# Turning a decoder's tokens through DRAM and VectorE's 32x32 squares, and the last step of a norm on GpSimd

## The chip, the cores and the metric

The kernel runs on one core of a Trainium2 chip. The metric is the device time of one execution in microseconds (us). Five engines work side by side, each with its own queue of instructions in a fixed order: TensorE (PE in the profile; its weight loads are PEld), VectorE (DVE), ScalarE (ACT), GpSimd (POOL) and SyncE (SP), which here issues nearly all DMAs. An engine's instruction waits until what it needs from others is there, and all that stands behind it in its queue waits too.

## The reference

Two decoder layers on 16 sequences of 128 tokens, 512 features wide, in float32. Each sublayer is followed by a sum and a norm without weights:

```python
x = _layernorm(x + _L0_attn_ref(x, ...))            # softmax attention, 16 heads over 4 key heads, rotary
x = _layernorm(x + _L0_xattn_ref(x, ctx_512, ...))  # latent cross attention, 16 heads of 128
x = _layernorm(x + _L0_ffn_ref(x, w1, w2, w3))      # gated FFN with ternary weights, 1408 wide
x = _layernorm(x + _L1_attn_ref(x, ...))            # lightning (decay) attention, 16 heads of 32
x = _layernorm(x + _L1_xattn_ref(x, ctx_512, ...))  # causal softmax cross attention, 16 heads of 32
x = _layernorm(x + _L1_ffn_ref(x, ...))             # 8 experts, two for each token, and a shared expert

def _layernorm(x, axis=-1, eps=1e-05):
    m = jnp.mean(x, axis=axis, keepdims=True)
    v = jnp.var(x, axis=axis, keepdims=True)
    return (x - m) / jnp.sqrt(v + eps)
```

## The kernel before

**Tiling.** The tokens stay in on-chip memory through all six stages as 16 tiles `x[b]` ("blocks") of 128 tokens by 512 features, tokens on the partitions. A projection contracts over features, so it needs them on the partitions: a block is turned into four squares of 128x128, written `xT[:, k, at : at + P]`, k being 0 to 3. Blocks go in groups of four (`GB = 4`, `NG = 4` groups); `xT` holds a group, 4 x 512 values on each partition. Before the change every block is turned by four TensorE transposes into a bank of PSUM and one ACT copy out of it (`transpose_x`, L125 to L130; stage 3 has its own at L673).

**Stages and their order.**

- *Stage 1*, softmax self attention. `attend` (L229) runs over the blocks, n counting up: scores of block n on TensorE; their softmax, where VectorE takes maxima (L188), ACT the exponentials (L193), GpSimd the division (L200); the turning of the probabilities of block n - 1 on TensorE (L205) with a copy by VectorE (L207); values and output projection of block n - 2 (`project_out`, L146). The projections of the next group are a list of tasks with costs in microseconds, made by `prepare(g)`; a `Share` deals them out between these steps by their cost, so that TensorE has them to do while it waits for a softmax. `prepare` also appends `folds`: products of cross attention weights of stage 2, whose raw tensors (`raw`, 1.7 MB each) come by SP.
- *Stage 2*, latent cross attention, runs over (group, half of the heads, block). `context` (L535) fetches a group's latent keys and values from DRAM (`rep`, from `dkv`, which `rotate` wrote), turns them and the group's tokens; `project` makes queries and keys for a half; `Heads` does softmax and values. Ternary weights of stage 3 are made in between (`pieces`).
- *Stage 3*, the FFN. For each group, 11 chunks f of hidden units: 16 matmuls (L697) with the tokens split into a high and a low part (`xh`, `xl`), then the product with the third matrix. The turning of the next group (`inputs`, `one`) hangs in a list `todo`, one item in each chunk.
- *Stage 4*, decay attention. For each group: turning, eight pieces of queries and keys (L785), values (L793); then each block goes through a `Pipeline` of scores, values and `project_out`.
- *Stage 5*, softmax cross attention, is `attend` again, with its own `prepare` (L891). It also loads shared weights for stage 6, and at its start has SP write 20 MB of zeros to DRAM (`slots_x`, `sums`, L900).
- *Stage 6*, the experts, is not touched.

**Norm.** `statistics` (L110) takes mean and variance on VectorE, and the reciprocal root on GpSimd (L116, L118); `layernorm` then has VectorE do the last step (L123). `project_out` of stages 1, 4 and 5 calls it, and so do stages 2 and 3.

Order within an engine is the program's, unless a scheduler moves an instruction that is ready sooner; `tc.keep_in_program_order` forbids that for one instruction. Tiles with the same `tag` share `bufs` rooms: a new tile waits until the oldest has been read for the last time.

Of the kernel before, what the change touches and what calls it, by code (L numbers as in the profile page):

```python
# [12 lines left out]
F32 = mybir.dt.float32  # L13
F32R = mybir.dt.float32r
AF = mybir.ActivationFunctionType
ALU = mybir.AluOpType
# [29 lines left out]
def decoder_kernel(ctx: ExitStack, tc: tile.TileContext, a: dict, out: bass.AP):  # L46
# [71 lines left out]
        nc.gpsimd.tensor_tensor(rstd, ve, nhalf, ALU.pow)  # L118
        return mv[:, 0:1], rstd

    def layernorm(b):
        mean, rstd = statistics(b)
        nc.vector.tensor_scalar(x[b], x[b], mean, rstd, ALU.subtract, ALU.mult)  # L123

    def transpose_x(xT, b, at):  # L125

        tr = bank("mm", [P, KC, P], "tr")
        for k in range(KC):
            nc.tensor.transpose(tr[:, k, :], x[b][:, k * P : (k + 1) * P], ident)
        nc.scalar.copy(xT[:, :, at : at + P], tr)  # L130

    def chain(tasks, name, pairs, then):

# [179 lines left out]
    with tc.tile_pool(name="p1", bufs=1) as p1:  # L313
# [85 lines left out]
        def prepare(g):  # L399
            if g == NG:  # L400
                room = p1.tile([P, KC, TG], F32, tag="xT", name="room")
                ct, t2 = (room[:, n].rearrange("p (b d) -> p b d", d=DC) for n in range(2))
                return [(0, rotate(0, ct, kvr0, t2))] + folds(2, LATE)
            xT = p1.tile([P, KC, TG], F32, tag="xT", name="xT")
            qkT = p1.tile([P, 5, TG], F32, tag="qkT", name="qkT", bufs=2)
            v = p1.tile([P, GB, P], F32, tag="v", name="v", bufs=2)
            groups[g] = qkT, v
            tasks = []

            def turn(i):  # L410
# [3 lines left out]
            tasks += [(0.64, lambda i=i: turn(i)) for i in range(GB)]  # L414
# [92 lines left out]
    with tc.tile_pool(name="p2", bufs=1, reuse_waits="tile") as p2:  # L507
# [27 lines left out]
        def context(g, kvr):  # L535
            reps = []
            for i in range(GB):
                rep = p2.tile([P, 4, DC], F32, tag="rep", name="rep", bufs=GB + 1)
                for qi in range(4):
                    nc.sync.dma_start(  # L540
                        rep[qi * Q : (qi + 1) * Q], dkv[g * GB + i].rearrange("(kj k) d -> k kj d", k=Q)
                    )
                reps.append(rep)
            pk = bank("mm", [P, GB, P], "pk")
            for i in range(GB):
                nc.tensor.transpose(pk[:, i, :], kvr[:, i, :], ident)
            kvT = p2.tile([P, TG], F32, tag="kvT", name="kvT")
            nc.scalar.copy(kvT, pk.rearrange("p b l -> p (b l)"))
            xT = p2.tile([P, KC, TG], F32, tag="xT", name="xT")
            for i in range(GB):  # L550
                transpose_x(xT, g * GB + i, i * P)
            return xT, kvT, reps

        def project(xT, kvT, half):
            qT = p2.tile([P, 4, TG], F32, tag="qT", name="qT")
# [65 lines left out]
                    if self.half == 1:  # L621
                        layernorm(self.b)

        kvr = kvr0
# [7 lines left out]
        for m in range(len(steps) + 2):  # L632
            if m < len(steps):
                g, half, i = steps[m]
                if i == 0:
                    if half == 0:
                        xT, kvT, reps = context(g, kvr)
# [5 lines left out]
                if (half, i) == (1, 1) and g + 1 < NG:  # L643
                    kvr = p2.tile([P, GB, DC], F32, tag="kvr", name="kvr")
                    rotate(g + 1, room("ct"), kvr, room("t2"))()
# [17 lines left out]
    with tc.tile_pool(name="p3", bufs=1) as p3:  # L663
        w1, w2 = (tern.w[n].rearrange("p (k f) -> p k f", k=KC) for n in range(2))
        def inputs(g):
            xh = p3.tile([P, KC, TG], F32R, tag="xh", name="xh", bufs=2)
            xl = p3.tile([P, KC, TG], F32R, tag="xl", name="xl", bufs=2)

            def one(i):
                at = slice(i * P, (i + 1) * P)  # L670
                tr = bank("mm", [P, KC, P], "tr")
                for k in range(KC):
                    nc.tensor.transpose(tr[:, k, :], x[g * GB + i][:, k * P : (k + 1) * P], ident)  # L673
                nc.scalar.copy(xh[:, :, at], tr)
                nc.vector.tensor_tensor(xl[:, :, at], tr, xh[:, :, at], ALU.subtract)
            return (xh, xl), [lambda i=i: one(i) for i in range(GB)]

        xs, todo = inputs(0)
        for run in todo:
# [4 lines left out]
        for g in range(NG):  # L684
# [51 lines left out]
    with tc.tile_pool(name="p4", bufs=1) as p4:  # L736
# [28 lines left out]


        pipe = Pipeline((0, 1, 2))
        for g in range(NG):
            xT = p4.tile([P, KC, TG], F32, tag="xT", name="xT", bufs=2)
            for i in range(GB):  # L770
                transpose_x(xT, g * GB + i, i * P)
                nc.gpsimd.tensor_tensor(x[g * GB + i], x[g * GB + i], bo4, ALU.add)
            if g == 0:
                for j in range(4):
                    dj = p4.tile([P, 4, P], F32, tag=f"dec{j}", name=f"dec{j}")
                    for c in range(4):
                        h = 4 * c + j
                        nc.scalar.activation(dj[:, c, :], diff, AF.Exp, scale=nsl[:, h : h + 1])
                    nc.gpsimd.tensor_tensor(dj, dj, bc(maskT, 4), ALU.mult)
                    dec.append(dj)  # L780
            qkT = p4.tile([P, 8, TG], F32, tag="qkT", name="qkT", bufs=2)
            for c in range(8):
                pq = bank("mm", [P, TG], "pq")
                for k in range(KC):
                    nc.tensor.matmul(  # L785
                        pq, lhsT=wq4[k // 2][:, k % 2, c * P : (c + 1) * P], rhs=xT[:, k, :], start=(k == 0), stop=(k == KC - 1)
                    )
                nc.scalar.activation(qkT[:, c, :], pq, AF.Identity, bias=bcol[:, c : c + 1])
            vs = []
            for i in range(GB):  # L790
                pv = bank("mm", [P, D], "pv")
# [5 lines left out]
                v = p4.tile([P, D], F32, tag="v", name="v", bufs=6)  # L797
                nc.vector.tensor_tensor(v, pv, bv4, ALU.add)
                vs.append(v)
            for i in range(GB):  # L800
                toks = slice(i * P, (i + 1) * P)
                mine = {}

# [67 lines left out]
    with tc.tile_pool(name="p5", bufs=1) as p5:  # L871
# [12 lines left out]
        nc.gpsimd.iota(count[:, NC + NB :], [[P, NT]], base=NB * P, channel_multiplier=1)  # L884
        ramp = moe.tile([P, NC + NB + NT], F32, tag="ramp", name="ramp")
        nc.vector.tensor_copy(ramp, count)
        wq5, wo5 = wqo5[:, 0], wqo5[:, 1]
        psum.share(mm=2, sc=4, pt=2)
        groups = {}

        def prepare(g):  # L891
# [12 lines left out]
            xT = p5.tile([P, KC, TG], F32, tag="xT", name="xT", bufs=2)  # L904
# [22 lines left out]
            for i in range(GB):  # L927
                chain(
                    tasks, "pv", [(ctT[:, i * P : (i + 1) * P], wkv5[:, D : 2 * D])],
                    lambda pv, i=i: nc.scalar.copy(vs[i], pv),  # L930
                )
            return tasks

        def score(sc, n):
# [487 lines left out]
```

## Time and profile before

| | us |
|---|---|
| median of three runs (lowest, highest) | 2133.3 (2128.42, 2134.7) |
| the profiled execution | 2133.8 |
| its span, first to last instruction | 2132.0 |
| TensorE's mean granted clock in it, as a share of full speed | 0.991 |
| stage 1, self attention | 0 to 266 |
| stage 2, latent cross attention | 266 to 767 |
| stage 3, FFN | 767 to 1021 |
| stage 4, decay attention | 1021 to 1291 |
| stage 5, softmax cross attention | 1291 to 1546 |
| stage 6, experts | 1546 to 2132 |

The ends of stages are read from the timeline and are good to a microsecond or two, as neighbouring stages overlap. In the profile's lines, "x64" counts instructions, "128x512 f32" is partitions by elements, and a bracket such as `[1.63 <-POOL rstd L118]` is the idle time of that engine just before the instruction and what ended it. L123 is line 123 of the kernel before. Of the lines that concern the turning: L129, TensorE's transposes of tokens outside stage 3, 320 instructions of 273 ns (they overlap one another); L673, the same in stage 3, 64 instructions; L130, ACT's copy of a turned block, 80 of 585 ns; L123, the norm's last step, 80 of 547 ns at the median.

### The profile page before, as it was taken

Reading aid. Unit: us, or ns where it says so; the run is one execution under the profiler, and the core shown is the slowest. Engines: PE = TensorE matmul, PEld = TensorE weight load, DVE = VectorE, ACT = ScalarE, POOL = GpSimd, SP = SyncE. Lnnn points to the kernel's source line nnn. Section 1 sums busy time; section 2 is a strip of 40 time slices with the busy share of each in tenths; the row PEclk is TensorE's granted clock in tenths of the full one; section 3 lists DMA queues with packets and bytes.
Section 4 is the critical chain, followed back from the end, with each engine's and each line's share of the span. In section 5 each row is a group of like instructions: output and inputs, shape, how many; then the busy total and the mean of one; then the engine's idle time right before and its main releaser. Section 6 shows DMA issues by size and latency. Waiting matters only on the chain.

```text
span 2132.0 us, 26951 instructions
## 1 busy us (share of the span) xinstructions
PE 2077.3 (97%) x10273; PEld 1170.9 (55%) x10273; DVE 865.6 (41%) x1776; ACT 642.6 (30%) x2252; POOL 540.9 (25%) x626
## 2 busy tenths in 40 slices
PE   8999999999999999999999999999799999999998
PEld 5555554445454468888455544555444455555553
DVE  4677733444554343322124424677631122222224
ACT  4555533323333322222211113566431111111112
POOL 5443321211111122222211101333303212222223
PEclk9999999999999999999999999999899999999999
DMA  6001220212220010001200029300004268999874
GB/s 227 1 34 44 103 85 22 63 46 70 60 70 1 1 54 1 1 1 60 93 1 1 1 50 301 140 21 21 26 16 164 83 214 293 292 298 304 297 216 165
DMA packets 82896, 210.05 MB, mean 99 GB/s; under 512 B 19792, under 2 KB 38096, under 8 KB 76112
## 3 DMA queue, kind: packets, MB, share of 16 engines
q0 software_dynamic: 13792, 105.55, 15.1%
q1 hardware_dynamic: 67872, 101.47, 14.5%
q8 instruction: 81, 1.33, 0.3%
q10 hardware_dynamic: 1104, 1.31, 0.2%
q14 instruction: 47, 0.39, 0.1%
HBM read 159.70 MB, written 48.61 MB: 98 GB/s over the span
## 4 chain that ended last, share of the span: by engine, by line
PE 90%; DVE 4%; DMA 2%; ACT 1%; POOL 1%; issue 1%; ACTq 0%; POOLq 0%; DVEq 0%; SPq 0%
PE po L615 11%; PE po L150 8%; PE pq L139 6%; PE pq L561 5%; PE pq L785 5%; PE ry L1182 4%; PE rg L1161 4%; PE ru L1161 4%; PE pg L1050 4%; PE pa L697 4%; PE pb L697 4%; PE po L724 4%; PE po L139 3%; PE pu L1050 3%; PE av L602 3%; PE pv L793 3%
## 5 line engine op out<-in xcount | busy, mean ns | idle before, releaser
L200 POOL TENSOR_TENSOR p<-p,rs 128x512 f32<-128x512 f32 x192 | 200.9, 1046 | 582.8 <-DVE rs L199 550.6
L615 PE MATMUL po<-mT,cc 128*128 128x512 f32 x512 | 236.0, 605 | 0.0
L193 ACT ACTIVATE p<-t,nmx 128x128 f32<-128x128 f32 x512 | 198.6, 390 | 54.8 <-DVE nmx L188 24.7
L615 PEld LDWEIGHTS po<-mT,cc 128*128 128x128 f32 x512 | 92.2, 189 | 107.2 <-issue 103.6
L193 ACT ACTIVATE p<-sc,nmx 128x128 f32<-128x128 f32 x256 | 90.0, 372 | 147.5 <-DVE nmx L188 142.1
L561 PE MATMUL pq<-xT,wqr 128*128 128x512 f32 x256 | 117.5, 602 | 1.0 <-ACT xT L130 0.7
L150 PE MATMUL po<-wo,oT 128*128 128x512 f32 x256 | 117.1, 601 | 0.4 <-ACT qkT L418 0.4
L785 PE MATMUL pq<-xT,wq 128*128 128x512 f32 x256 | 110.9, 594 | 1.0 <-ACT xT L130 0.7
L116 POOL TENSOR_SCALAR ve<-mv 128x1 f32<-128x1 f32 x80 | 18.0, 225 | 366.1 <-DVE mv L114 351.3
L1182 PE MATMUL ry<-ew,ractT 128*128 128x512 f32 (+1 forms) x234 | 106.9, 592 | 0.0
L1161 PE MATMUL rg<-ew,xsT 128*128 128x352 f32 x312 | 99.2, 461 | 3.5 <-DMA ew<-in_l1f_w_dram,which 3.5
L1161 PE MATMUL ru<-ew,xsT 128*128 128x352 f32 x312 | 98.7, 459 | 0.0
L193 ACT ACTIVATION_READ_ACCUMULATOR p<-t,nmx 128x1 f32 x512 | 96.3, 188 | 0.0
L205 PEld LDWEIGHTS pt<-ident,p 128*128 128x128 f32 x512 | 60.5, 143 | 62.3 <-issue 54.9
L1135 POOL DMA_INDIRECT ew<-in_l1f_w_dram,which x39 | 38.0, 973 | 213.0 <-PE ry L1182 184.6
L205 PE MATMUL pt<-ident,p 128*128 128x128 f32 x512 | 80.4, 281 | 10.1 <-DVE pT L207 6.8
L708 POOL TENSOR_TENSOR hl<-ht,hh 128x512 fp32r<-128x512 f32 x44 | 60.3, 1371 | 114.8 <-ACT hh L706 114.8
L1168 DVE TENSOR_TENSOR ract<-rsg,ru 128x352 f32<-128x352 f32 x39 | 20.3, 521 | 168.9 <-PE ru L1161 168.9
L207 DVE COPY pT<-pt 128x512 f32<-128x512 f32 x128 | 86.5, 678 | 4.7 <-PE pt L205 4.4
L123 DVE TENSOR_SCALAR x<-x,mv,rstd 128x512 f32<-128x512 f32 x80 | 51.0, 638 | 91.0 <-POOL rstd L118 91.0
L1050 PE MATMUL pg<-xT,sw_gu 128*128 128x512 f32 x192 | 86.5, 593 | 0.0
L188 DVE TENSOR_REDUCE nmx<-t 128x4 f32<-128x512 f32 x128 | 84.0, 675 | 0.8
(234 smaller groups left out, 3658.9 us busy)
## 6 DMA issues: line engine op xcount, KB each, us to landing
piece<-in_l0f_w_dram SPq DMA_DIRECT2D x48, 352.0 KB, 3.2
raw<-in_l0x_raw_dram SPq DMA_DIRECT2D x8, 1728.0 KB, 7.4
slots_x<-zero SPq DMA_DIRECT2D x1, 10062.0 KB, 29.4
xs<-slots_x SPq DMA_DIRECT2D x39, 258.0 KB, 9.0
sums<-zero SPq DMA_DIRECT2D x1, 9984.0 KB
rep<-dkv SPq DMA_DIRECT2D x64, 64.0 KB, 2.0
sums<-x SPq DMA_DIRECT2D x16, 256.0 KB, 2.0
sum<-sums SPq DMA_DIRECT2D x16, 256.0 KB, 4.9
```

What stands on the lines that cost most here:

```text
L139: nc.tensor.matmul(got["p"], lhsT=lhsT, rhs=rhs, start=(n == 0), stop=(n == len(pairs) - 1))
L150: nc.tensor.matmul(po, lhsT=oT[:, c, :], rhs=wo[:, c, :], start=(c == 0), stop=(c == KC - 1))
L193: nc.scalar.activation(self.p[:, j, :], src[:, j, :], AF.Exp, bias=nmx[:, j : j + 1], accum_out=self.sm[:, j : j + 1])
L200: nc.gpsimd.tensor_tensor(self.p, self.p, spread(rs, P), ALU.mult)
L205: nc.tensor.transpose(pt[:, j, :], self.p[:, j, :], ident)
L561: nc.tensor.matmul(pq, lhsT=wqr[:, k, cols], rhs=xT[:, k, :], start=(k == 0), stop=(k == KC - 1))
L615: nc.tensor.matmul(self.po, lhsT=self.cc[:, 4 * par + j, :], rhs=mT[h], start=(par == 0 and j == 0), stop=(par == 1 and j == 3),)
L697: nc.tensor.matmul(dst, lhsT=wt[:, k, f * P : (f + 1) * P], rhs=xs[n][:, k, :], start=(k == 0 and n == 0), stop=(k == KC - 1 and n == 1),)
L785: nc.tensor.matmul(pq, lhsT=wq4[k // 2][:, k % 2, c * P : (c + 1) * P], rhs=xT[:, k, :], start=(k == 0), stop=(k == KC - 1))
L1050: nc.tensor.matmul(dst, lhsT=sw_gu[:, k, at : at + P], rhs=xTs[g][:, k, :], start=(k == 0), stop=(k == KC - 1),)
L1161: nc.tensor.matmul(dst, lhsT=self.xT[:, k, :], rhs=gu[:, k, off : off + FE], start=(k == 0), stop=(k == KC - 1),)
L1182: nc.tensor.matmul(po, lhsT=self.actT[:mw, m_, :], rhs=dn[:mw, m_, :], start=(m_ == 0), stop=(m_ == 2))
```

## The change

Of each group after the first in stages 2 to 5, and of groups 2 and 3 in stage 1, the blocks are turned without TensorE. A class `Turn` does it in three steps. `send`: ACT copies the block with its features regrouped, so that each partition holds, for each quarter q, 4 x 32 features (`xp`), and SP writes that to a DRAM tensor `turned`. `fetch`: SP reads it back by four DMAs, one for each q, in runs of 128 values, so that partition (q, r) gets row r of each square row of quarter q (`x2`). `back`: one VectorE instruction transposes all 32x32 squares and puts them in `xT`. In stage 1 the tokens come from the input, so `turned` is filled for groups 2 and 3 straight from `x` in DRAM, by eight DMAs issued after the loads of `x`.

`project_out` has GpSimd do the last step of its norm. Stages 2 and 3 keep it on VectorE.

Around this, steps move: in stage 1 the folds come interleaved with the turning of groups 2 and 3; in stage 2 the rotation of the next group's context comes one step earlier, and `kvr` has one room; in stage 3 the list has nine items for a group, several in one chunk where needed; in stage 4 sends go between the pieces of queries and keys and backs ahead of blocks 0 and 2; in stage 5 the five steps of a group's turning are put among the tasks of the group before.

```diff
-    def layernorm(b):
+    def layernorm(b, engine=nc.vector):
         mean, rstd = statistics(b)
-        nc.vector.tensor_scalar(x[b], x[b], mean, rstd, ALU.subtract, ALU.mult)
+        engine.tensor_scalar(x[b], x[b], mean, rstd, ALU.subtract, ALU.mult)
...
+    turned = dram.tile([NB, P, D], F32, tag="turned", name="turned")
+    QP = P // 4
+
+    class Turn:
...
+        def send(self, pool, tag="xp"):
+            xp = pool.tile([P, 4, KC, QP], F32, tag=tag, name="xp")
+            nc.scalar.copy(xp, x[self.b].rearrange("p (k q a) -> p q k a", k=KC, q=4))
+            nc.sync.dma_start(turned[self.b], xp.rearrange("p q k a -> p (q k a)"))
+
+        def fetch(self, pool, tag="x2", bufs=1):
+            self.x2 = pool.tile([P, 4, P], F32, tag=tag, name="x2", bufs=bufs)
+            rows = turned[self.b].rearrange("(t r) (q f) -> q r t f", r=QP, q=4)
+            for q in range(4):
+                nc.sync.dma_start(self.x2[q * QP : (q + 1) * QP], rows[q])
+
+        def back(self, xT):
+            tc.keep_in_program_order(nc.vector.transpose(
+                xT.rearrange("p k (t r) -> p t k r", r=QP), self.x2.rearrange("p t (k a) -> p t k a", k=KC)
+            ))
...
-        layernorm(b)
+        layernorm(b, nc.gpsimd)
```

Stage 1:

```diff
         load_x(GB, NB)
+        for g in range(2, NG):
+            blocks = slice(g * GB, (g + 1) * GB)
+            for k in range(KC):
+                nc.sync.dma_start(
+                    turned[blocks].rearrange("n p (q k a) -> (n p) q k a", q=4, k=KC)[:, :, k, :],
+                    a["x"][blocks].rearrange("n p (k q a) -> (n p) k q a", q=4, k=KC)[:, k],
+                )
...
             def turn(i):
-                transpose_x(xT, g * GB + i, i * P)
+                if g < 2:
+                    transpose_x(xT, g * GB + i, i * P)
+                else:
+                    mine = Turn(g * GB + i)
+                    mine.fetch(p1, bufs=3)
+                    mine.back(xT[:, :, i * P : (i + 1) * P])
...
-            return tasks + (folds(g - 2, g - 1) if g >= 2 else [])
+
+            first = folds(g - 2, g - 1) if g >= 2 else []
+            for i in range(GB):
+                first.insert(2 * i, tasks[i])
+            return first + tasks[GB:]
```

Stages 2, 3 and 4:

```diff
+        def send2(blocks):
+            sent = [Turn(b) for b in blocks]
+            for t in sent:
+                t.send(p2, "t2")
+                t.fetch(p2, "ct" if t.b % GB == 2 else "x2")
+            return sent
...
+                if g + 1 < NG:
+                    if (half, i) == (0, 3):
+                        sent = send2([(g + 1) * GB])
+                    if (half, i) == (1, 0):
+                        rotate(g + 1, room("ct"), kvr0, room("t2"))()
+                        xT = p2.tile([P, KC, TG], F32, tag="xT", name="xT")
+                    if half == 1 and i >= 1:
+                        for t in sent:
+                            j = t.b % GB
+                            t.back(xT[:, :, j * P : (j + 1) * P])
+                        sent = send2([(g + 1) * GB + j for j in ((), (1, 2), (3,), ())[i]])
...
+            order = [(sent, 0), (sent, 1), (one, 0), (sent, 2), (one, 1), (sent, 3), (one, 2), (None, 0), (one, 3)]
+            return (xh, xl), [lambda f=f, i=i: f and f(i) for f, i in order]
...
-                if f and todo:
+                for _ in range(-(-len(todo) // (NF0 - f)) if f else 0):
                     todo.pop(0)()
...
+                if c in (2, 4) and g + 1 < NG:
+                    send4((g + 1) * GB + c // 2 - 1)
...
             for i in range(GB):
+                if i in (0, 2) and g + 1 < NG:
+                    for n in (i, i + 1):
+                        coming.pop(0).back(xT[:, :, n * P : (n + 1) * P])
+                        if i == 0:
+                            send4((g + 1) * GB + 2 + n)
```

Stage 5, in `prepare(g)`:

```diff
-            tasks += [(0.64, lambda i=i: transpose_x(xT, g * GB + i, i * P)) for i in range(GB)]
+            if g == 0:
+                tasks += [(0.64, lambda i=i: transpose_x(xT, i, i * P)) for i in range(GB)]
...
+            if g + 1 < NG:
+
+                xTn = p5.tile([P, KC, TG], F32, tag="xT", name="xT", bufs=2)
+                turned5.append(xTn)
+                turns = [Turn((g + 1) * GB + i) for i in range(GB)]
+
+                def step(n):
+                    if n:
+                        turns[n - 1].back(xTn[:, :, (n - 1) * P : n * P])
+                    if n < GB:
+                        turns[n].send(p5)
+                        turns[n].fetch(p5)
+
+                for n in reversed(range(GB + 1)):
+                    tasks.insert(len(tasks) - 4 * (GB + 1 - n), (0, lambda n=n: step(n)))
```

More of the change, by code (lines that the diff above doesn't have):

```diff
@@ L130, in transpose_x, with __init__ @@
         nc.scalar.copy(xT[:, :, at : at + P], tr)
+    turned = dram.tile([NB, P, D], F32, tag="turned", name="turned")
+    QP = P // 4
+    class Turn:
+        def __init__(self, b):
+            self.b = b
+        def send(self, pool, tag="xp"):
[11 more added lines that the diff above has]
+            ))
     def chain(tasks, name, pairs, then):
@@ L410, in turn @@
             def turn(i):
-                transpose_x(xT, g * GB + i, i * P)
+                if g < 2:
[4 more added lines that the diff above has]
+                    mine.back(xT[:, :, i * P : (i + 1) * P])
                 nc.gpsimd.tensor_tensor(x[g * GB + i], x[g * GB + i], bo, ALU.add)
-            tasks += [(0.64, lambda i=i: turn(i)) for i in range(GB)]
+            tasks += [(0.0 if g >= 2 else 0.64, lambda i=i: turn(i)) for i in range(GB)]
             for c in range(5):
@@ L548, in context @@
             nc.scalar.copy(kvT, pk.rearrange("p b l -> p (b l)"))
[L549 to L552, printed above, removed]
+            return kvT, reps
         def project(xT, kvT, half):
@@ L622, in out @@
                         layernorm(self.b)
-        kvr = kvr0
+        def send2(blocks):
[4 more added lines that the diff above has]
+            return sent
         late = []
@@ L636, in decoder_kernel @@
                     if half == 0:
-                        xT, kvT, reps = context(g, kvr)
+                        kvT, reps = context(g, kvr0)
+                        if g == 0:
+                            xT = p2.tile([P, KC, TG], F32, tag="xT", name="xT")
+                            for j in range(GB):
+                                transpose_x(xT, j, j * P)
                     qT, kT = project(xT, kvT, half)
@@ L642, in decoder_kernel @@
                 held[m].turn()
-                if (half, i) == (1, 1) and g + 1 < NG:
-                    kvr = p2.tile([P, GB, DC], F32, tag="kvr", name="kvr")
-                    rotate(g + 1, room("ct"), kvr, room("t2"))()
+                if g + 1 < NG:
[3 more added lines that the diff above has]
+                        rotate(g + 1, room("ct"), kvr0, room("t2"))()
+                        xT = p2.tile([P, KC, TG], F32, tag="xT", name="xT")
+                    if half == 1 and i >= 1:
[3 more added lines that the diff above has]
+                        sent = send2([(g + 1) * GB + j for j in ((), (1, 2), (3,), ())[i]])
             if m >= 2:
@@ L667, in inputs, with sent @@
             xl = p3.tile([P, KC, TG], F32R, tag="xl", name="xl", bufs=2)
+            turns = [Turn(g * GB + i) for i in range(GB)]
+            def sent(i):
+                turns[i].send(p3)
+                turns[i].fetch(p3, bufs=2)
             def one(i):
                 at = slice(i * P, (i + 1) * P)
-                tr = bank("mm", [P, KC, P], "tr")
-                for k in range(KC):
-                    nc.tensor.transpose(tr[:, k, :], x[g * GB + i][:, k * P : (k + 1) * P], ident)
+                if g == 0:
+                    tr = bank("mm", [P, KC, P], "tr")
+                    for k in range(KC):
+                        nc.tensor.transpose(tr[:, k, :], x[i][:, k * P : (k + 1) * P], ident)
+                else:
+                    tr = p3.tile([P, KC, P], F32, tag="xT", name="xT")
+                    turns[i].back(tr)
                 nc.scalar.copy(xh[:, :, at], tr)
                 nc.vector.tensor_tensor(xl[:, :, at], tr, xh[:, :, at], ALU.subtract)
-            return (xh, xl), [lambda i=i: one(i) for i in range(GB)]
+            if g == 0:
+                return (xh, xl), [lambda i=i: one(i) for i in range(GB)]
+            order = [(sent, 0), (sent, 1), (one, 0), (sent, 2), (one, 1), (sent, 3), (one, 2), (None, 0), (one, 3)]
+            return (xh, xl), [lambda f=f, i=i: f and f(i) for f, i in order]
         xs, todo = inputs(0)
@@ L767, in decoder_kernel, with send4 @@
         pipe = Pipeline((0, 1, 2))
+        coming = []
+        def send4(b):
+            coming.append(Turn(b))
+            coming[-1].send(p4)
+            coming[-1].fetch(p4, bufs=2)
+            nc.gpsimd.tensor_tensor(x[b], x[b], bo4, ALU.add)
         for g in range(NG):
[L769 to L772, printed above, removed]
             if g == 0:
+                xT = p4.tile([P, KC, TG], F32, tag="xT", name="xT")
+                for i in range(GB):
+                    transpose_x(xT, i, i * P)
+                    nc.gpsimd.tensor_tensor(x[i], x[i], bo4, ALU.add)
                 for j in range(4):
@@ L799, in decoder_kernel @@
                 vs.append(v)
+            if g + 1 < NG:
+                xT = p4.tile([P, KC, TG], F32, tag="xT", name="xT")
             for i in range(GB):
+                if i in (0, 2) and g + 1 < NG:
[3 more added lines that the diff above has]
+                            send4((g + 1) * GB + 2 + n)
                 toks = slice(i * P, (i + 1) * P)
@@ L886, in decoder_kernel @@
         nc.vector.tensor_copy(ramp, count)
+        turned5 = []
         wq5, wo5 = wqo5[:, 0], wqo5[:, 1]
@@ L903, in prepare @@
             ctT = p5.tile([P, TG], F32, tag="ctT", name="ctT", bufs=2)
-            xT = p5.tile([P, KC, TG], F32, tag="xT", name="xT", bufs=2)
+            xT = turned5.pop(0) if g else p5.tile([P, KC, TG], F32, tag="xT", name="xT", bufs=2)
             qT = p5.tile([P, KC, TG], F32, tag="qT", name="qT", bufs=2)
@@ L916, in prepare @@
             tasks = [(0.64, turn_context)]
-            tasks += [(0.64, lambda i=i: transpose_x(xT, g * GB + i, i * P)) for i in range(GB)]
+            if g == 0:
+                tasks += [(0.64, lambda i=i: transpose_x(xT, i, i * P)) for i in range(GB)]
             for c in range(KC):
@@ L931, in prepare @@
                 )
+            if g + 1 < NG:
+                xTn = p5.tile([P, KC, TG], F32, tag="xT", name="xT", bufs=2)
[9 more added lines that the diff above has]
+                    tasks.insert(len(tasks) - 4 * (GB + 1 - n), (0, lambda n=n: step(n)))
             return tasks
```

## The prediction

> **What bounds the kernel now.** I read the page's busy times first, then the chain of waits' shares, then busy time stage by stage.
>
> ```profile
> PE 2077.3 (97%) x10273; PEld 1170.9 (55%) x10273; DVE 865.6 (41%) x1776; ACT 642.6 (30%) x2252; POOL 540.9 (25%) x626
> ...
> PE 90%; DVE 4%; DMA 2%; ACT 1%; POOL 1%; issue 1%; ACTq 0%; POOLq 0%; DVEq 0%; SPq 0%
> ```
> ```profile
> 0.00:266.00 266.00, 252.08 (x1567) 147.08 (x1567) 176.98 (x351) 140.81 (x577) 110.47 (x132) 0.99 0.23 82
> 266.00:767.00 501.00, 498.27 (x2530) 251.61 (x2528) 205.11 (x383) 161.11 (x692) 92.39 (x108) 1.00 0.15 45
> 767.00:1021.00 254.00, 250.50 (x1122) 206.66 (x1122) 86.44 (x140) 63.06 (x105) 72.95 (x76) 0.99 0.07 24
> 1021.00:1291.00 270.00, 267.37 (x1595) 133.08 (x1594) 84.58 (x144) 46.28 (x81) 34.34 (x56) 1.00 0.14 36
> 1291.00:1546.00 255.00, 237.60 (x1688) 132.19 (x1686) 170.71 (x343) 139.74 (x580) 79.49 (x99) 0.96 0.27 99
> ```
>
> The rows are stages 1 to 5 (stage 6, the experts, keeps its transposes); the columns after the length are busy PE, PEld, DVE, ACT, POOL, then granted clock, DMA share, GB/s. TensorE bounds every stage, so each microsecond of transpose removed is one gained, unless what replaces it is late. Only stage 5 has slack to speak of (17.4 us), and there a second cause shows, near its end:
>
> ```profile
> 1503.45 0.17 DVE L114 BATCH_NORM_AGGREGATE mv<-st 128x2 f32<-128x6 f32 x1
> ...
> 1505.28 0.57 POOL L118 TENSOR_TENSOR rstd<-ve,nhalf 128x1 f32<-128x1 f32 x1
> 1505.88 0.55 DVE L123 TENSOR_SCALAR x<-x,mv,rstd 128x512 f32<-128x512 f32 x1 [1.63 <-POOL rstd L118]
> ```
>
> VectorE waits 1.63 us for GpSimd's `rstd`, then spends 0.55 us, while the softmax stands behind it in its queue.
>
> **Transposes removed.** 56 blocks lose four transposes each: 8 in stage 1 (groups 2, 3), 12 in each of stages 2 to 5. The timeline of TensorE prices one block:
>
> ```profile
> 385.75 1.09 PE L129 MATMUL tr<-ident,x 128*128 128x128 f32 x8
> 386.78 0.69 PE L602 MATMUL av<-pT,rep 32*128 32x256 f32 x2
> ```
>
> Two blocks, start to next start, 1.03 us: 0.52 a block in stage 2, so 12 x 0.52 = 6.2. In stage 1 the same reading (84.94 to 85.81) gives 0.44: 8 x 0.44 = 3.5. In stage 3 a chunk with them takes 4.12 us (801.59 to 805.71), one without about 3.65: 12 x 0.47 = 5.6. In stage 4 four blocks take 0.53 + 1.02 + 0.59 = 2.1 (1084.70 on): 3 x 2.1 = 6.3. Stage 5 at 0.45: 12 x 0.45 = 5.4. **Sum 27.0 us.**
>
> A rule speaks against it: the Trainium skill, "VectorE: DVE Perf Modes", section "Rules for kernel authors", sends a 128x128 transpose to TensorE if PSUM can take it, since VectorE turns only 32x32 squares. The row agrees that VectorE is slower: its transpose of 128x512 (L592) takes 711 ns, plus a copy by ACT (0.58, as `xT`'s L130), against 0.44 to 0.52. By the rule, with VectorE's turn standing on the path as TensorE's did, 56 blocks lose 56 x (0.71 - 0.5) = 12 us; by the rows of the stages the work goes from a 97% engine to one of 41% and 27 us are gained. I take the rows. ACT's new copy replaces L130, so in stages 2 to 5 ACT issues as much as before; in stage 1 it loses 8.
>
> **What must hide, stages 2 to 4.** Each block adds a 256 KB write and four 64 KB reads on SP's queue. Near rows: `sums<-x` (256 KB) lands in 2.0 us; `rep<-dkv` (64 KB, same runs of 512 B) takes 0.43 us to issue and lands in 2.0. So a block's round trip is 0.6 copy + 2.0 to 2.5 + 4 x 0.43 + 2.0 + 0.7 turn, about 7 us, and 4 to 5 in series once copies overlap. SP's fetches wait for their write, and what is queued on SP behind them (stage 2: `rep`, `dkv`) waits too. Stage 2 sends a step of 15 us ahead: hidden; without it, 7 us per group. Stage 3 has 15 items over 10 chunks instead of one each; VectorE and ACT (86 and 63 us busy in 254) fit. Stage 4: `send4` follows projection pieces c = 2 and 4, the two backs come before block 0's decay products in VectorE's queue; I charge 0.5 us a group, 1.5 in all (bounds 0 and 9, three exposed fetches).
>
> **Stage 1's prefill.** Eight DRAM to DRAM copies, 256 KB each in pieces of 128 B: 16,384 pieces, 1,024 for each DMA engine. They stand on SP's queue from about 23.4 us, ahead of `wkr` and the first `raw`, and the fetches of group 2 wait for them. VectorE's first back sits where block 8 is due, and the fold that is moved ahead needs `raw` there as well: 86 us (1.75 MB, 4.4 us at 400 GB/s, behind the copies; a fetch 3). No row writes DRAM in such pieces. The nearest: 1270 to 1286, pieces of 256 B, 10579 packets in 16 us at a full DMA share, 16 x 16 x 1.09 / 10579 = 26 ns per packet. The Trainium skill, "DMA: Bandwidth & Descriptors", section "Specifications", says that below 512 B the engine reads, modifies and writes. By the row 1,024 x 26 = 27 us, over at 51; if that trebles or quadruples by the rule, 80 to 105 us, over at 104 to 129, and VectorE stands 25 to 50 us. It is late from 53 ns on. I take the row, with 3 us for the doubt.
>
> **GpSimd's last norm step** (48 blocks of stages 1, 4, 5). A tensor operation of 128x512 on GpSimd takes 1.05 to 1.13 us (L200, L412), so about 1.1; its bounds are 0.6 and 1.4. GpSimd is idle three quarters of the time, L200 at worst waits 1 us. VectorE is relieved of 2.2 us a block where it is what TensorE waits for: in stage 5's last blocks (L123 at 1493.56, 1505.88, 1518.95, 1532.01) 4 x 2.2 = 8.8, I take 8; in stage 1 one stall of 2.64 us before `pt`, which ends on VectorE's queue behind such a wait, I take 2.2. The last block's norm is longer by 0.5. **Together +9.7.**
>
> **Stage 5's first hand-over.**
>
> ```profile
> 1294.81 0.38 SPq L900 DMA_DIRECT2D slots_x<-zero  x1
> 1295.24 17.83 SPq L900 DMA_DIRECT2D sums<-zero  x1
> 1313.17 31.73 SPq L760 DMA_DIRECT2D ct<-in_ctx_dram  x2
> ```
>
> 20 MB of zeros fill SP's queue until about 1350 (the windows show 373 GB/s to 1350, 88 after). The stage begins at 1290.5; block 4's write stands behind them. Then come four blocks with one `xp` and one `x2` between them, in series: 4 x 4.5 = 18 us, so the group is turned at about 1290.5 + 60 + 18 = 1368. The order of the changed program puts the softmax of blocks 0 to 3 ahead of these backs on VectorE, and on TensorE only that is left to do. First scores at 1318.9, then some 11 us of VectorE a block (7.6 softmax, 1.5 sum and statistics, the rest waits): done at about 1352. So TensorE stands 16 us, less the 4 it stood there before: **-12** (bounds 0, if the writes overtake the zeros, and -30, at 9 us a block). Groups 2 and 3 have 50 us for their 18.
>
> **Sum.** 27.0 + 9.7 - 1.5 - 3 - 12 - 0.5 = 19.7 from the profiled execution's own 2133.8 (span 2132.0 and 1.8 around it): 2114.1. The median of the runs, 2133.3, is 0.5 lower, which I leave out.
>
> **Rivals.**
> *No hand-over is late* (0.27): the DMA queue lets the writes through or TensorE has enough to do, and the prefill costs nothing. For it: DMA share is 0.06 to 0.3 nearly everywhere. Against: the 17.8 and 31.7 us for which SP itself was held. 2114 - 15 = 2099.
> *The prefill is late* (0.24), slower: 90 ns a piece, 92 us, over at 116, with `raw` and a fetch 123 against 86: 37 us of VectorE and TensorE idle. 2114 + 3 + 37 = 2154, and the other costs as in my sum. It makes the kernel slower by more than what can be told from 26 us of stall on (79 ns a piece). For it: SP's single queue, the rule, both ends in DRAM; against: the row of 26 ns.
> *Given back* (0.08): stage 5's chain costs 9 us a block, -30 instead of -12: 2132.
> *The turning does not leave TensorE's queue*: excluded, TensorE has 224 transposes fewer in the order of the changed program.
>
> **How the numbers follow.** About 0.3% (6.4 us) can be told from no change. My forecast (0.41) and the first rival are faster: 0.68; same 0.08; slower 0.24. The likeliest is 2114, its own range 2104 to 2124; the range for 8 in 10 takes in the first rival from below and most of the prefill's from above: 2095 to 2152.
>
> **What would show it.** Chunks of stage 3 all about 3.65 us; stage 4's groups shorter by 2; L123 on GpSimd near 1.1 us and no 1.6 us wait of VectorE ahead of the softmax in stage 5; an idle stretch of TensorE of 10 to 20 us near 1350 ended by VectorE's turn; eight `turned<-in_x` DMAs over by 55. A first back in stage 1 later than 90, or TensorE standing in each group of stages 2 to 4, would prove me wrong.

## The result and the profile after

The changed kernel takes 2138.5 us (median of 20 runs, 2132.0 to 2146.4) against 2133.3 for the kernel before (20 runs, 2127.3 to 2136.9): ratio 1.0029, 95% interval 1.0018 to 1.0040. It is a little slower, where 2114 was forecast. The profiled execution has a span of 2137.4 us. First its page: TensorE's busy time, its granted clock in 40 slices, and the chain of waits.

```profile
PE 2061.9 (96%) x10049; PEld 1156.9 (54%) x10049; DVE 873.9 (41%) x1784; ACT 647.4 (30%) x2256; POOL 638.4 (30%) x674
...
PEclk9999999999999999999999998799999999999999
...
PE 86%; DMA 5%; DVE 4%; POOL 2%; issue 1%; ACT 1%; SPq 1%; ACTq 0%; POOLq 0%; DVEq 0%
...
L123 POOL TENSOR_SCALAR x<-x,mv,rstd 128x512 f32<-128x512 f32 x48 | 100.6, 2095 | 4.5
```

224 matmul instructions are gone and TensorE is 15.4 us less busy, yet the span is 5.4 us longer. DMA has grown from 2% to 5% of the chain, and the clock has a dip to 7 tenths in the 26th slice. The norm's step on GpSimd takes 2095 ns.

Stage by stage, from the first matmul that only that stage has to the first of the next (one profiled execution each):

| stage | before | changed | difference | forecast |
|---|---|---|---|---|
| 1 self attention | 271.0 | 261.8 | -9.2 | -2.7 |
| 2 latent cross attention | 502.2 | 507.0 | +4.8 | -6.2 |
| 3 FFN | 251.4 | 244.5 | -6.9 | -5.6 |
| 4 decay attention | 269.4 | 263.2 | -6.2 | -4.8 |
| 5 softmax cross attention | 257.7 | 275.3 | +17.6 | -0.9 |
| 6 experts | 580.3 | 585.6 | +5.3 | 0 |

Up to the end of stage 4 the changed kernel is 17.5 us ahead. Stage 5 gives all of it back. Busy time by stage in the changed kernel, with the columns of the prediction's table:

```profile
768.80:1013.30 244.50, 243.28 (x1072) 200.98 (x1072) 100.59 (x150) 69.62 (x118) 69.79 (x76) 0.99 0.15 48
1013.30:1276.50 263.20, 261.72 (x1536) 129.39 (x1537) 80.72 (x140) 43.89 (x76) 64.49 (x71) 0.99 0.22 60
1276.50:1551.80 275.30, 244.48 (x1667) 138.43 (x1666) 165.77 (x337) 144.68 (x587) 116.89 (x117) 0.91 0.32 116
```

Stages 3 and 4 are as full as they were and simply shorter. In stage 5 TensorE is idle for 30.8 us, and its clock, 0.96 before, is 0.91. The timeline of SP's queue there, then VectorE's turns, then TensorE:

```profile
1279.08 21.07 SPq L990 DMA_DIRECT2D sums<-zero  x1
1300.27 25.97 SPq L146 DMA_DIRECT2D turned<-xp  x1
1326.65 2.76 SPq L832 DMA_DIRECT2D ct<-in_ctx_dram  x2
1335.34 2.24 SPq L152 DMA_DIRECT2D x<-turned  x4
```
```profile
1341.59 0.71 DVE L155 STREAM_TRANSPOSE xT<-x 128x512 f32<-128x512 f32 x1
1347.43 0.71 DVE L155 STREAM_TRANSPOSE xT<-x 128x512 f32<-128x512 f32 x1 [5.13 <-DMA x<-turned]
1351.63 0.71 DVE L155 STREAM_TRANSPOSE xT<-x 128x512 f32<-128x512 f32 x1 [3.49 <-DMA x<-turned]
1355.74 0.71 DVE L155 STREAM_TRANSPOSE xT<-x 128x512 f32<-128x512 f32 x1 [3.41 <-DMA x<-turned]
```
```profile
1356.51 6.62 PE L166 MATMUL pq<-xT,wqo 128*128 128x512 f32 x8 [15.58 <-DVE xT L155]
...
1363.82 3.69 PE L166 MATMUL pq<-xT,wqo 128*128 128x512 f32 x8
```

SP needs 25.97 us to issue the write of block 4, because the queue in front of it is full of zeros. The read follows at 1335; the second block comes 5.8 us after the first, the others 4.2 us apart. TensorE waits 15.58 us for the last of them. Then the same eight matmuls that take 3.69 us at full clock take 6.62.

### The profile page after: what moved, and what is told of

Its sections match the earlier page's. It is cut to its first block, busy times and chain, and to the rows that moved or that the text cites. A ratio compares the mean times of both kernels' runs of the same rounds, so it can differ in the third digit from the quotient of the medians.

```text
span 2137.4 us, 27152 instructions
## 1 busy us (share of the span) xinstructions
PE 2061.9 (96%) x10049; PEld 1156.9 (54%) x10049; DVE 873.9 (41%) x1784; ACT 647.4 (30%) x2256; POOL 638.4 (30%) x674
## 4 chain that ended last, share of the span: by engine, by line
PE 86%; DMA 5%; DVE 4%; POOL 2%; issue 1%; ACT 1%; SPq 1%; ACTq 0%; POOLq 0%; DVEq 0%
PE po L655 9%; PE po L177 7%; PE pq L166 6%; PE pq L865 5%; PE pq L601 5%; PE ry L1288 4%; PE pg L1156 4%; PE pa L769 4%; PE pb L769 4%; PE rg L1267 4%; PE po L796 4%; PE ru L1267 4%; DMA ew<-in_l1f_w_dram,which 3%; PE pu L1156 3%; PE po L166 3%; PE pv L875 3%
## 5 line engine op out<-in xcount | busy, mean ns | idle before, releaser
L227 POOL TENSOR_TENSOR p<-p,rs 128x512 f32<-128x512 f32 x192 | 200.7, 1046 | 501.1 <-DVE rs L226 466.5
L601 PE MATMUL pq<-xT,wqr 128*128 128x512 f32 x256 | 121.8, 620 | 1.6 <-ACT xT L130 0.7
L123 POOL TENSOR_SCALAR x<-x,mv,rstd 128x512 f32<-128x512 f32 x48 | 100.6, 2095 | 4.5
L1300 POOL DMA_INDIRECT sums<-ry,place x39 | 62.0, 1590 | 90.9 <-DMA sums<-ry,place 42.2
```

Source lines behind the costliest of these rows:

```text
L227: nc.gpsimd.tensor_tensor(self.p, self.p, spread(rs, P), ALU.mult)
L601: nc.tensor.matmul(pq, lhsT=wqr[:, k, cols], rhs=xT[:, k, :], start=(k == 0), stop=(k == KC - 1))
```

## The experiments

All are timed beside the kernel before on the same chip. "Theory 1" is the hand-over in stage 5 behind the zeros; its rivals are named in the expectations, which stand as written before each run.

| kernel | us | ratio to before (95%) | stages 1 to 6 in its profile |
|---|---|---|---|
| norm_alone | 2112.6 | 0.9904 (0.9882 to 0.9926) | 265.5, 502.5, 250.9, 269.4, 239.3, 581.4 |
| turn_alone | 2164.0 | 1.0139 (1.0113 to 1.0164) | 267.6, 509.4, 244.7, 265.5, 289.3, 586.5 |
| s5_tensor | 2102.9 | 0.9858 (0.9835 to 0.9882) | 262.5, 508.0, 244.6, 263.2, 240.4, 581.8 |
| s5_zeros_early | 2121.6 | 0.9948 (0.9928 to 0.9967) | 261.8, 507.0, 272.0, 263.0, 233.1, 579.8 |
| zeros_stage4 | 2114.7 | 0.9918 (0.9904 to 0.9932) | 262.2, 507.6, 244.7, 281.0, 233.1, 583.7 |
| zeros4_s2_tensor | 2109.0 | 0.9890 (0.9873 to 0.9908) | 262.4, 502.1, 245.7, 281.3, 233.3, 583.0 |
| zeros4_norm_all | 2111.5 | 0.9906 (0.9889 to 0.9923) | 262.9, 503.9, 244.7, 281.3, 233.1, 583.3 |
| zeros4_s1_tensor | 2116.8 | 0.9933 (0.9918 to 0.9947) | 266.9, 507.6, 244.8, 281.1, 233.7, 579.6 |
| zeros_kept | 2096.7 | 0.9835 (0.9817 to 0.9852) | 262.9, 506.2, 245.6, 263.5, 234.5, 584.6 |
| kept_s2_tensor | 2088.0 | 0.9793 (0.9777 to 0.9809) | 261.7, 502.3, 245.4, 263.3, 234.2, 581.4 |
| kept_s2_norm | 2087.0 | 0.9785 (0.9767 to 0.9802) | 263.0, 500.9, 244.6, 263.3, 234.2, 584.6 |

### The two halves of the change apart

norm_alone is the kernel before with this edit; turn_alone is the changed kernel without it.

```diff
-        layernorm(b)
+        layernorm(b, nc.gpsimd)
```

> The kernel before with GpSimd taking the last norm step of project_out, nothing else. Theory 1 (stage 5's first hand-over is what ate the gain; the norm on GpSimd helps although it takes 2.1 us instead of 0.55): stage 1 shorter by 3 to 6 us, stage 5 by 4 to 8, together 2121 to 2127. Theory 2 (the norm on GpSimd is the loss, since 2.1 us stand ahead of the softmax divisions on GpSimd): no gain or slower, 2133 to 2145, with waits of TensorE for p on GpSimd.

> The changed kernel with the last norm step back on VectorE. Theory 1: slower than the changed kernel by what norm_alone gains, 2144 to 2152. Theory 2: faster than it, 2125 to 2134.

The norm alone gains 21.7 us (2134.3 on that chip to 2112.6), turning alone loses 29.7. Theory 2 falls: the 2.1 us on GpSimd cost nothing that shows, and without them the changed kernel is 25 us slower still. But theory 1's numbers were too small on both sides. Stage 5 of the two kernels that differ by the norm only (first row the kernel before, second norm_alone; columns as above):

```profile
1294.00:1551.70 257.70, 239.82 (x1715) 134.52 (x1714) 170.30 (x342) 143.20 (x587) 79.49 (x99) 0.96 0.27 99
```
```profile
1288.00:1527.60 239.60, 229.50 (x1717) 129.97 (x1716) 159.10 (x325) 142.91 (x587) 116.88 (x117) 1.00 0.29 107
```

The same matmuls, 10.3 us less busy: they ran at full clock, where the kernel before had 0.96. Idle time fell from 17.9 to 10.1 us. Of the 18 us gained, the larger half is clock. The start of each block's output projection, counted from the stage's first scores, tells where: block 3 at 66 us instead of 71, block 11 at 169 instead of 177, block 15 at 204 instead of 221. So about 9 us come in the last four blocks, and 8 before. The clock in the records is full or half: the kernel before has half clock (0.50) from 1372.5 to 1379.3 and in four stretches of 3.4 us in the last blocks. TensorE works 20.2 us in these, so half clock costs 10.1 us, which is the busy time that norm_alone saves. TensorE's waits of 1.8 to 3.0 us in this stage are gone there too; the longest left is 0.92.

### Stage 5's hand-over

s5_tensor takes stage 5's turning back to TensorE and leaves out the steps of `Turn`; s5_zeros_early keeps them, and puts the zeros at the end of stage 3 in the program instead of the start of stage 5.

```diff
-            if g == 0:
-                tasks += [(0.64, lambda i=i: transpose_x(xT, i, i * P)) for i in range(GB)]
+            tasks += [(0.64, lambda i=i: transpose_x(xT, g * GB + i, i * P)) for i in range(GB)]
...
```
```diff
                     wq4.append(t)
+                zero = p3.tile([P, D + 4], F32, tag="zero", name="zero")
+                nc.gpsimd.memset(zero, 0.0)
+                for t, rows, width in ((slots_x, NT, D + 4), (sums[NB * P :], NT, D)):
+                    nc.sync.dma_start(
...
```

> The changed kernel with stage 5 turned by TensorE as before. Theory 1: the idle 15.6 us and the slow clock around it go, stage 5 falls from 278 us to 250 to 258, total 2112 to 2120. Theory 2: stage 5 stays over 268, total 2130 or more.

> The changed kernel with the 20 MB of zeros written from the end of stage 3 on, after that stage's last fetch. Theory 1 (the zeros on SP's queue delay the hand-over): group 1 of stage 5 is turned before its first softmax is over, TensorE does not wait for xT, total 2106 to 2115. Theory 3 (one room each for xp and x2, and the place of the turns in VectorE's queue delay it): TensorE still waits 8 us or more for xT, total 2125 to 2138.

Both take stage 5 from 275.3 us to less than the kernel before had: 240.4 with TensorE, some ten less than the least that was expected, and 233.1 with the turning kept and the zeros gone. With the same turns, the same single rooms and the same order, TensorE no longer waits for `xT`; theory 3 falls. The row of stage 5 in s5_zeros_early, against the last of the three rows of the changed kernel:

```profile
1303.80:1536.90 233.10, 223.36 (x1668) 125.09 (x1667) 165.59 (x337) 143.87 (x587) 116.35 (x116) 1.00 0.14 49
```

Instructions are 1668 against 1667. Idle time is 9.7 against 30.8 us, 21 less; busy time is 223.4 against 244.5, another 21, at clock 1.00 against 0.91. So the zeros cost this stage 42 us, half of it as idle time and half as longer busy time, most of that from the slow clock.

The total missed its expectation by 7 us, and stage 3 says why: it is 272.0 us long instead of 244.5. The zeros did not go out at the stage's end, where the program has them: the scheduler drew them forward to 764.4 and 808.4 us, the stage's start, ahead of loads of the FFN's third matrix. SP takes 19.34 us over two of these (at 811.07), and TensorE's largest wait in that kernel is now there:

```profile
PE po L806 <- DVE ffn_w L546: 23.1, 1, 23.1
```

### Finding a place for the zeros

zeros_stage4 issues them at the last group of stage 4. zeros_kept does the same and pins the two DMAs to program order.

```diff
+            if g == NG - 1:
+                zero = p4.tile([P, D + 4], F32, tag="zero", name="zero")
+                nc.gpsimd.memset(zero, 0.0)
+                for t, rows, width in ((slots_x, NT, D + 4), (sums[NB * P :], NT, D)):
+                    nc.sync.dma_start(
...
```
```diff
-                    nc.sync.dma_start(
+                    tc.keep_in_program_order(nc.sync.dma_start(
...
```

> The changed kernel with the 20 MB of zeros written from the start of stage 4's last group, behind that stage's last fetch and ahead of stage 5. Theory 1 (zeros ahead of the first write of stage 5 are its whole loss): stage 5 about 233 us as in s5_zeros_early, stages 3 and 4 as in the changed kernel (244.5 and 263), total 2088 to 2097. Rival (the zeros harm wherever they are): stage 4 or 5 longer by 10 or more, total over 2105.

> zeros_stage4 with the two DMAs of zeros held in program order, so that they come behind stage 4's last fetch and not ahead of it. Theory 1: no TensorE wait for xT in stage 4 or 5, stage 4 falls from 281 to about 263, stage 5 stays at 233, total 2092 to 2099. Rival (a stage loses wherever 20 MB are in flight): stage 4 stays above 270.

zeros_stage4 missed by 18 us: stage 4 took 281.0 instead of 263, as the rival said. But the scheduler had drawn the zeros forward, since nothing holds them, from the last group of stage 4 to the first, ahead of the reads for the second group. SP's lines there and TensorE's largest wait:

```profile
1017.46 2.31 SPq L869 DMA_DIRECT2D slots_x<-zero  x1
1029.84 20.00 SPq L152 DMA_DIRECT2D x<-turned  x4
...
1050.58 0.66 SPq L869 DMA_DIRECT2D sums<-zero  x1
1058.42 20.73 SPq L152 DMA_DIRECT2D x<-turned  x4
```
```profile
PE pq L876 <- DVE xT L155: 14.2, 1, 14.2
```

It is theory 1 in another stage, unplanned: twice SP takes 20 us over four reads, which take it 1.75 us in zeros_kept (at 1030.08), and TensorE stands for the turned tokens until 1093.8. Pinned, the zeros come at 1188, behind the last read, and stages 3, 4 and 5 are at 245.6, 263.5 and 234.5 together for the first time. The rival, that 20 MB in flight slow a stage wherever they are, falls: during them stage 4 takes what it took without.

### Stage 2

zeros4_s2_tensor gives the turning of stage 2 back to TensorE and the context's rotation its old place and room; zeros4_norm_all instead leaves the turning and changes one line:

```diff
+                if (half, i) == (1, 1) and g + 1 < NG:
+                    kvr = p2.tile([P, GB, DC], F32, tag="kvr", name="kvr")
+                    rotate(g + 1, room("ct"), kvr, room("t2"))()
...
```
```diff
-    def layernorm(b, engine=nc.vector):
+    def layernorm(b, engine=nc.gpsimd):
```

> zeros_stage4 with stage 2 turned by TensorE and its context rotated where it was before. Theory 4 (in stage 2 the context's DMA waits for a room that the turning shares, GpSimd stands for it ahead of rstd, VectorE ahead of the softmax): stage 2 falls from 507 to about 502, total 4 to 6 us below zeros_stage4. Rival: stage 2 stays at 506 or more.

> zeros_stage4 with the last norm step on GpSimd in stages 2 and 3 too. Theory 4: VectorE no longer stands behind rstd, so stage 2 falls to 497 to 502 though GpSimd still waits for the context; total 5 to 10 us below zeros_stage4. Rival (GpSimd's own divisions are what comes late): stage 2 unchanged within 2 us.

Stage 2 falls from 507.6 to 502.1 with TensorE turning, and to 503.9 with the norm's step on GpSimd; totals fall by 5.8 and 3.2. The first is as expected. The second's are a third to two thirds of what was expected. The changed kernel's timeline around the second group's start, from GpSimd, VectorE and TensorE:

```profile
371.75 0.72 POOL L415 TENSOR_TENSOR t<-ct,s 128x256 f32<-128x256 f32 x1 [6.75 <-DMA rep<-dkv]
...
373.44 0.57 POOL L118 TENSOR_TENSOR rstd<-ve,nhalf 128x1 f32<-128x1 f32 x1
```
```profile
374.04 0.55 DVE L123 TENSOR_SCALAR x<-x,mv,rstd 128x512 f32<-128x512 f32 x1 [4.33 <-POOL rstd L118]
```
```profile
380.79 0.67 PE L642 MATMUL av<-pT,rep 32*128 32x256 f32 x2 [2.59 <-DVE pT L632]
381.86 5.40 PE L601 MATMUL pq<-xT,wqr 128*128 128x512 f32 x8 [0.41 <-DVE x L660]
387.10 1.02 PE L604 MATMUL pk<-kvT,wkr 128*128 128x512 f32 x2
387.95 3.68 PE L601 MATMUL pq<-xT,wqr 128*128 128x512 f32 x8
```

GpSimd stands 6.75 us for the context's DMA with `rstd` behind it in its queue. (The releaser's name, `rep<-dkv`, is the DMA that came last by the profile; L415 reads `ct`, and SP issued that load at 368.21.) In the kernel before, the same load held GpSimd 1.4 us in all of stage 2. VectorE stands 4.33 us for `rstd` with the softmax behind it; TensorE stands 2.59 us for the softmax, and its next eight matmuls take 5.40 us instead of 3.68. At the third group the same waits are 7.30, 5.08 and 3.34 us. That the load is late because it shares a room with the turning, rather than because of its place on SP's queue, was not taken apart: no run gives it a room of its own or leaves the rotation where it was.

### Stage 1

zeros4_s1_tensor has stage 1 turned by TensorE, without the copies in DRAM.

```diff
-        for g in range(2, NG):
-            blocks = slice(g * GB, (g + 1) * GB)
...
-                if g < 2:
-                    transpose_x(xT, g * GB + i, i * P)
-                else:
...
+                transpose_x(xT, g * GB + i, i * P)
```

> zeros_stage4 with stage 1 turned by TensorE, without the copies in DRAM and with the folds where they were. If the copies of 128 B pieces cost nothing: stage 1 about 265.5 as in norm_alone, total 3 to 5 us above zeros_stage4. If they cost what the sum charged (3 us): no more than 1 us above it.

Stage 1 is 4.7 us longer (266.9 against 262.2). The totals differ by 2.1 us only, and their runs overlap (2111.9 to 2116.6, and 2114.9 to 2120.8); stage 6, which the edit doesn't touch, was 4.1 us shorter in this profile. By the stage the copies cost nothing; the totals alone don't decide it.

### The best of these

> zeros_kept with stage 2 turned by TensorE. From zeros4_s2_tensor: 5 us below zeros_kept, 2087 to 2093.

> kept_s2_tensor with the last norm step on GpSimd in stages 2 and 3 too. If the wait for the context was the only thing that made the norm matter in stage 2: within 2 us of kept_s2_tensor. If the norm matters there by itself: 3 us or more below it, 2084 to 2089.

Turning by VectorE in stages 1, 3, 4 and 5, by TensorE in stage 2, with the zeros behind stage 4's last read, takes 2088.0 us: ratio 0.9793 (0.9777 to 0.9809), about 2% faster than the kernel before and faster than the changed one. The step from zeros_kept is 8.7 us in the medians, of which stage 2 shows 3.9 and stage 6, which the edit doesn't touch, 3.2. The norm on GpSimd in stages 2 and 3 adds nothing that these runs can tell (2087.0); stage 2 itself goes from 502.3 to 500.9.

## Why the prediction was wrong

Its own sums first: the 0.5 us of the last block's norm were taken off twice, so that 19.7 should have been 20.2; and the rival of the prefill adds the 3 us that 2114 already holds, so that 2154 should have been 2148. That is not what failed.

**Transposes removed: right where nothing came late.** Forecast 5.6 and 4.8 for stages 3 and 4, measured 6.9 and 6.2. In stage 5, 5.4 forecast, and s5_tensor against s5_zeros_early differ by 7.3, though the place of the zeros differs too. In stage 1, 3.5 forecast and 4.7 by zeros4_s1_tensor. The rows carried it, not the Trainium skill's rule ("VectorE: DVE Perf Modes", section "Rules for kernel authors") that sends such transposes to TensorE. In stage 2 TensorE was the better place, but because of a late load, of which that rule says nothing.

**"Stage 2 sends a step of 15 us ahead: hidden": failed.** The turned tokens did arrive in time. What came late was a load and a chain of three queues that the move of the rotation had brought together: the context's load, GpSimd's `rstd` behind it, VectorE's softmax behind that. The prediction costed the added DMAs as transfers, and named SP's queue, but it did not ask who stands behind the instruction that waits for the moved load. Instead of a gain of 6.2, a loss of 4.8. The 11.0 between them are in the trace: TensorE's two waits make 5.9, and the 9.7 us of work that it did at half clock behind them (382.8 to 386.2 and 505.7 to 512.5) cost 4.9.

**The prefill: the row was even too high, and the 3 us too many.** 16,384 pieces were a doubt with 37 us in the rival. In the changed kernel VectorE's first back, at 86.77 us, has no idle time ahead of it. From 24 to 42 us the hardware queue moved 17054 packets with 93.6% of 16 engines: 0.936 x 16 x 18 / 17054 = 16 ns a packet, for 26 in the row. Under 512 B were 16531 of them, so the copies were nearly over by 42, for 51 in the forecast. The Trainium skill, "DMA: Bandwidth & Descriptors", section "Specifications", says of such pieces that they are read, modified and written; it gives no factor; three or four was the prediction's own, and no price of it shows here.

**GpSimd's step: mis-sized, without harm.** Forecast 1.1 us with bounds of 0.6 and 1.4; it takes 2.1. The rows used, L200 and L412, do one operation on each element; L123 does two, a subtraction and a product. That this is why it takes twice as long was not tested. It is hidden as forecast.

**What the norm is worth: mis-sized.** The term was 9.7 and it measures 21.7. The 8 us for the last four blocks came out (about 9), but some 5 of these are half clock, which the term did not have; the 2.2 of stage 1 were 5.5. What was missing is the price of short waits in the first twelve blocks of stage 5, and the clock: 10 of stage 5's 18 us are matmuls that were slow after such waits.

**"TensorE stands 16 us, less the 4 it stood there before: -12": the step that decided.** The wait was 15.58 us, but in part by luck. Counted from the stage's first scores, the group was turned after 55 us, where 49 were forecast, and TensorE's other work lasted 39 us, where 33 were (33 is three blocks at 11 us, though four were named); the two misses cancel. And the price of the wait was wrong: the cost is 42 us. TensorE's time was taken as its wait, while what it does before and after also became slower. The changed kernel's stage 5, with busy TensorE and clock, cut where the clock changes:

```profile
1301.60:1311.20 9.60, 7.71 (x80) 5.68 (x79) 7.66 (x16) 7.16 (x33) 2.61 (x3) 1.00 1.05 389
1311.20:1324.90 13.70, 13.70 (x82) 10.93 (x84) 8.47 (x19) 8.56 (x43) 5.70 (x6) 0.50 1.04 397
1324.90:1335.10 10.20, 7.83 (x82) 5.88 (x78) 9.68 (x22) 7.98 (x40) 4.65 (x5) 1.00 1.02 352
1335.10:1362.40 27.30, 10.00 (x47) 5.34 (x48) 6.36 (x12) 7.56 (x26) 3.66 (x4) 0.50 0.35 113
1362.40:1390.00 27.60, 27.09 (x100) 11.98 (x98) 7.67 (x14) 9.09 (x16) 2.89 (x3) 1.00 0.27 92
```

From 1301.6 to 1340 there was no projection of group 1 to fill TensorE's gaps between softmaxes, since its tokens were not turned; it was idle 6 us in small pieces, and its clock fell to half twice. With two stretches of 3.4 us near the stage's end (from 1529.7 and 1539.9), TensorE worked 30.3 us at half clock: 15 of the 21 us of longer busy time. What the other 6 are is not shown.

The Trainium skill, "TensorE: Matmul & The Clock Gate", section "What's actually happening", says that the clock halves once TensorE has been idle for about 3.4 us and returns after as long at work. By that rule only the work behind the wait of 15.58 us is slow, for 3.4 us, and the loss is 1.7 us (an estimate from the page's figure). The trace agrees that the clock is half behind that wait, but it returned only after 5.9 us of work (1356.5 to 1362.4). And it had halved at 1311.2 and 1335.1, before the wait, when the records show no gap over 0.90 us (up to 1311.2) or 1.33 us (up to 1335.1); in stage 2 it halved after waits of 2.59 and 3.34 us. What sets it off in such stretches these runs don't show. The bound of -30 in the text came from another cause, 9 us a block, and even that was too small.

**Rivals.** The one given 0.08, that stage 5 gives the gain back and the result is 2132, was nearest in place, with another mechanism. The prefill, which got 0.24, did not happen; the wide range of 2095 to 2152 reaches up to the measured time only to take it in. That the result is so near to no change is chance as well: the norm's 12 us more than forecast hide a part of what stages 2 and 5 lost.

Stage 6 remains open. It was 580.3 us before and 585.6 after, but over thirteen profiles of kernels with the same stage 6 it lies between 579.6 and 586.5, and s5_zeros_early, which turns all the same blocks, has 579.8. The waits of TensorE for expert weights vary with it (2.3 to 8.5 us). It is not shown that the change causes it.

## What to carry to other kernels

A DMA that takes an engine's place brings that engine's deadline into a queue: look for the largest transfer ahead of it in the same queue, and move that one. A large write which nothing waits for belongs behind the last urgent read, and must be pinned there if a scheduler may draw it forward, as it did wherever the zeros were moved and not pinned. Whether another engine's queue for the turned tokens would have done as well was not tried. TensorE's idle time costs itself and the longer work around it; in this kernel's stage 5 that doubled the price.

## What the hardware showed unexpectedly

- The norm's last step, two operations with two values for each partition on 128x512 float32, takes 2.10 us on GpSimd and 0.55 on VectorE; a single product on that size (L227) takes 1.05 on GpSimd.
- SP is held by what it issues behind 20 MB of writes: 25.97 us for one write in the changed kernel, 20.00 for four reads in zeros_stage4, which take it 1.75 in zeros_kept.
- TensorE's clock halved in stretches where its longest recorded gap was 0.90 us (1301.6 to 1311.2), and in norm_alone and s5_zeros_early stage 5 ran at 1.00 throughout.
- DRAM to DRAM copies in pieces of 128 B went at about 16 ns a packet for each DMA engine; loads in pieces of 256 B at 26 (the prediction's row).
